# The place of two pairs' x loads on one core's DMA queue: four layers on a graph of 2048 nodes

## The chip, the core and the metric

The kernel runs on one core of a Trainium2 chip. Five engines work side by side, each through its own instructions in their written order, and wait for each other by semaphores: PE (TensorE, matrix products), DVE (VectorE), ACT (ScalarE), POOL (GpSimd) and SP (SyncE, which only issues transfers here). Transfers (DMAs) between the chip's memory (HBM) and the core's own memory (SBUF) are issued by SP, ACT or POOL and share 16 DMA engines. The metric is the device time of one execution in microseconds (us).

## The reference

Four layers work on `x`, of 8 batches x 2048 nodes x 64 channels, with one adjacency matrix `adj` of 2048 x 2048 (each row sums to 1). After each layer comes `x = layernorm(x + layer(x))`.

```python
# layer 0: node-wise weights made from an embedding of 16 numbers
w = einsum('nd,dkio->nkio', embedding, weight); b = einsum('nd,do->no', embedding, bias)
x_g = [x, adj @ x, 2 * adj @ (adj @ x) - x]          # k = 0, 1, 2
out = einsum('bnki,nkio->bno', x_g, w) + b
# layer 1: attention over the graph
e = leaky(s1[:, :, None] + s2[:, None, :]); att = softmax(where(adj > 0.5, e, -9e15))
out = elu(att @ x)
# layer 2: (adj + I) @ (x W^T + b) / degree
# layer 3: three steps of  v = relu([v, adj @ v] W1^T + b1) W2^T + b2
```

Everything is fp32. The host hands `adj` over twice, as it is (`adj`) and transposed (`adj_t`), and `x` with the nodes as rows.

## The kernel before

The 8 batches are four pairs; a pair's x is one SBUF buffer `SX[p]` of 128 partitions x 16 node tiles x 128 (two batches x 64 channels). It is loaded by `load_x(p, c, eng)` in four pieces of 256 KB, one for each quarter c of the nodes, and later overwritten by the results of each layer.

A product with adj is a sweep (`sweep`): for each of four column quarters, PE multiplies 16 tiles of a source by eight `a` tiles of adj (512 KB each), gathering in `acc`. The tiles come through a ring of six buffers; `fetch` issues the next load on SP when PE has let go of a buffer. Sweep 0 makes y1 = adj x for pairs 0 and 1. Sweep 1 makes adj y1 for pair 0 (`acc<-a,SA`). Sweep 2 does it for pair 1 (`acc<-a,SB`) and, with the same `a` tiles, makes y1 of pair 2 (`acc<-a,SX`): its first product, `first_product(2)`. Sweep 3 does the same for pairs 2 and 3. Later sweeps belong to layers 2 and 3.

Between the products stands the rest of layer 0: `second_pass` multiplies the stacked terms by the weights (`yp`; a group is six matmuls, for one node tile and one half of the 16 embedding numbers), and `add_terms` scales and adds the halves on ACT and DVE (`terms`). For pair 0 ACT takes the first half and DVE the second. PE can't begin a group before ACT or DVE has emptied the bank (PSUM) that it writes.

Beside all this the rows of adj go through the core once, for layer 1's mask and layer 2's degree: `rows_of_adj` loads 16 row tiles `an` of 1 MB on SP into a ring of four buffers; ACT sums each (L483), DVE makes the mask `mr` (L489) and POOL stores it (`by_row`).

`constants()` loads what is small, on SP: the first weights, then x of pairs 2 and 3 (`load_x` at L330, written by the helper's line L277 in the profile), then 17 small loads for layers 2 and 3 (L340 to L346: `w2bd`, `w31v`, `w31e`, `w32bd`, `w32c` twice each, `b2b`, `b32b`, `b31b` and `b32c` twice each, `ivc`). `weights_of_l23` makes the later weights from these on DVE, PE (`ps_w`) and ACT.

The order on every engine is fixed when the program is built. Each piece of work is a generator that yields the engine it needs next and what it waits for; a planner (`Plan`) holds an estimated time for each engine and for DMA and always goes on with the piece that can begin first by that estimate. `yield "PE", [180.0]` means: not before the planner's clock for this reaches 180. Planned times are close to the chip's, not equal: what is planned at 180 is issued on SP at 191.5 us. On the chip only semaphores hold; each engine goes through its list in order. SP's transfers use eight semaphores in turn, so that one issue waits for the landing of the eighth before it.

Of the kernel before, what the change touches and what calls it, by code (L numbers as in the profile page):

```python
# [20 lines left out]
NCH = 4  # L21
# [6 lines left out]
NPAIR = B // 2  # L28
# [125 lines left out]
def mm(cols, n=1):  # L154

    return n * max(4 * cols / 2390, 0.224)


def tr(n=1):
    return 0.11 * n  # L160
# [6 lines left out]
def act(n, k=1):  # L167
    return k * (n / 1220 + 0.14)
# [3 lines left out]
def resnorm_d4_kernel(  # L172
# [21 lines left out]
    nc = tc.nc  # L194
    plan = Plan()
    at = plan.at
# [27 lines left out]
    def tiny(shape, name, bufs=4):  # L224
        return wp.tile(shape, F32, tag=name, name=name, bufs=bufs)

    def tiles(c):
        return slice(c * TPC, (c + 1) * TPC)

    def cols(c):  # L230
        return slice(c * CW, (c + 1) * CW)
# [12 lines left out]
    SX = [slots.tile([P, NT, P], F32, name=f"SX{p}") for p in range(NPAIR)]  # L244
# [31 lines left out]
    def load_x(p, c, eng):  # L276
        eng.dma_start(  # L277
            SX[p][:, tiles(c), :],
            x[cols(c), p * P : (p + 1) * P].rearrange("(t p) n -> p t n", p=P),
        )  # L280
# [28 lines left out]
    def constants():  # L309

        yield "PE", [40.0]
        nc.sync.dma_start(emb_sb, emb.rearrange("(t p) d -> p t d", p=P))
        nc.sync.dma_start(bias_sb, bias0)
        nc.sync.dma_start(embT, emb_t)
        halves = [slice(0, C), slice(C, P)]
        for k, w in enumerate((wk0, wk1, wk2)):
            for h in halves:
                nc.sync.dma_start(w[h, :], w0[k * C : (k + 1) * C, :])
        for k in range(2):
            for e in range(2):  # L320
                nc.sync.dma_start(a4[halves[e], 2 * k + e : 2 * k + e + 1], a1[halves[k], :])
        yield "PE", [70.0]
        nc.vector.tensor_tensor(wk0, wk0, wk2, ALU.subtract)
        nc.vector.tensor_scalar_mul(wk2, wk2, 2.0)
        plan.run("DVE", 2.0)
        plan.start(0, embedding_bias())
        yield "PE", [180.0]
        for p in range(2, NPAIR):
            for c in range(NCH):
                load_x(p, c, nc.sync)  # L330
        yield "PE", [220.0]
        for t, src in (
            (w2bd, w2t),
            (w31v, w31t[0:C, :]),
            (w31e, w31t[C:P, :]),
            (w32bd, w32t),
            (w32c, w32t),
        ):
            for h in halves:
                nc.sync.dma_start(t[h, h], src)  # L340
        nc.sync.dma_start(b2b, b2.to_broadcast([P, C]))
        nc.sync.dma_start(b32b, b32.to_broadcast([P, C]))
        for h in halves:
            nc.sync.dma_start(b31b[h, :], b31)
            nc.sync.dma_start(b32c[h, :], b32.rearrange("o c -> c o"))
        nc.sync.dma_start(ivc, iv)  # L346
        yield "PE", [260.0]
        plan.start(0, weights_of_l23())

# [36 lines left out]
    def copy(eng, dst, src):  # L388
        (nc.scalar.copy if eng == "ACT" else nc.vector.tensor_copy)(dst, src)

    def cost(eng, n, k=1):
        return (act if eng == "ACT" else dve)(n, k)
# [11 lines left out]
    def embedding_bias():  # L404
        yield "PE", [pp_ring]
        pe, k = pp_ring.take([P, NT, C], "ps_eb")
        for t in range(NT):
            nc.tensor.matmul(
                pe[:, t, :], lhsT=embT[:, t * P : (t + 1) * P], rhs=bias_sb, start=True, stop=True
            )  # L410
        done = plan.run("PE", mm(C, NT))
        eng = yield EITHER, [done, e_ring]
        sb, ke = e_ring.take([P, NT, C], "eb_sb")
        copy(eng, sb, pe)
        done = plan.run(eng, cost(eng, 1024), done)
        pp_ring.give(k, done)
        e_ring.give(embT_k, plan.free["PE"])
        for e in range(2):
            nc.gpsimd.dma_start(eb[:, :, e, :], sb)
            done = plan.dma("DMA", 512, done)  # L420
        e_ring.give(ke, done)
        at["eb"] = done

    def weights_of_l23():


        yield "DVE", []
        for w, blocks in ((w2bd, 2), (w32c, 2), (b2b, 1), (b32b, 1)):
            mean = tiny([P, 1], "w_mean", 2)
            nc.vector.tensor_reduce(mean, w, AX.X, ALU.add)  # L430
            nc.vector.tensor_scalar_mul(mean, mean, 1.0 / C)
            for e in range(blocks):
                rows = slice(e * C, (e + 1) * C) if blocks == 2 else slice(0, P)
                block = w[rows, e * C : (e + 1) * C]
                nc.vector.tensor_scalar(block, block, mean[rows], None, ALU.subtract)
        plan.run("DVE", 3.0)

        nc.vector.tensor_tensor(w31v, w31v, w31e, ALU.subtract)

        yield "PE", [pp_ring, yt_ring]  # L440
        w32d, k2 = yt_ring.take([P, CW], "w32d")
        pw, k = pp_ring.take([P, CW], "ps_w")
        nc.tensor.transpose(pw[:, 0:P], w32bd, ident)
        nc.scalar.copy(w32d[:, 0:P], pw[:, 0:P])
        nc.vector.tensor_copy(w32d[:, P : 2 * P], b32c.to_broadcast([P, P]))
        done = plan.run("ACT", act(P), plan.run("PE", tr()))
        pp_ring.give(k, done)
        st_ring.give(w32bd_k, done)
        yield "PE", [pp_ring, done]
        pw, k = pp_ring.take([P, CW], "ps_w")  # L450
        for i, (lhs, rhs) in enumerate(
            [(w32d[:, 0:P], w31v), (w32d[:, 0:P], w31e), (w32d[:, P : 2 * P], w31e)]
        ):
            nc.tensor.matmul(
                pw[:, i * P : (i + 1) * P], lhsT=lhs, rhs=rhs, start=True, stop=True
            )
        nc.tensor.matmul(
            pw[:, 3 * P : 3 * P + 1], lhsT=w31v, rhs=b32c, start=True, stop=True
        )
        done = plan.run("PE", mm(P, 4))  # L460
        yield "ACT", [done]
        for i, dst in enumerate((gv, ge, ceb)):
            nc.scalar.copy(dst, pw[:, i * P : (i + 1) * P])
        nc.scalar.activation(b31n, pw[:, 3 * P : 3 * P + 1], AF.Identity, bias=b31b)
        done = plan.run("ACT", act(P, 4), done)
        pp_ring.give(k, done)
        yt_ring.give(k2, done)
# [93 lines left out]
    def y1_of(p):  # L561
        return (SA, SB)[p % 2]

    def y1_chunk(p, c, pa, ka, done):
        eng = yield EITHER, [done, yt_ring]
        yT, ky = yt_ring.take([P, CW], "y1T")
        copy(eng, yT, pa)
        done = plan.run(eng, cost(eng, CW), done)
        acc_ring.give(ka, done)
        nc.gpsimd.dma_start(y1_cols[p][:, cols(c)], yT)  # L570
        stored = plan.dma("DMA", 256, done)
        at["y1T", p, c] = stored
        yield "PE", [done, pp_ring]
        pt, k = pp_ring.take([P, TPC, P], "ps_y1")
        for j in range(TPC):
            nc.tensor.transpose(pt[:, j, :], yT[:, j * P : (j + 1) * P], ident)
        done = plan.run("PE", tr(TPC), done)
        yt_ring.give(ky, max(done, stored))
        eng = yield EITHER, [done]
        copy(eng, y1_of(p)[:, tiles(c), :], pt)  # L580
        done = plan.run(eng, cost(eng, CW), done)
        pp_ring.give(k, done)
        at["y1", p, c] = done
# [541 lines left out]
    def product(source, evict, need=None, before=None, seed=None):  # L1125
        return source, evict, need or (lambda q: []), before or (lambda c: []), seed
# [302 lines left out]
        at["joined", p] = 0.0  # L1429

    def first_product(p):
        return product(SX[p], lambda c, *a: y1_chunk(p, c, *a))

    def second_product(p):
        return product(
# [19 lines left out]
    def sweeps():  # L1455
# [13 lines left out]
        for s in range(3):  # L1469
            order_of_joint()  # L1470
        refill()
        yield from sweep(first_product(0), first_product(1), masks=True)
        for p in range(NPAIR):
            products = [second_product(p)]
            if 0 < p < NPAIR - 1:
                products.append(first_product(p + 1))
            if p == NPAIR - 1:
                yield from sweep(layer2_product(0))
                at["x1 used"] = 0.0
            yield from sweep(*products)  # L1480
# [16 lines left out]

    ctx.enter_context(tc.manual_schedule())
    plan.start(0, constants())
    plan.start(1, rows_of_adj())  # L1500
    plan.start(1, sums_of_a())
# [45 lines left out]
```

## Time and profile before

| what | value |
|---|---|
| median of three runs | 2073.46 us (2072.73 to 2073.87) |
| the profiled execution | 2070.24 us |
| its span, first to last instruction | 2068.5 us |
| mean granted clock of TensorE | 0.994 |
| DMA, whole span | 522.80 MB, mean 253 GB/s |

The profile is of one execution. Its span is cut into 40 slices; the clock granted to PE is 9 tenths or more in all of them, but within a slice it can fall to half for some microseconds. A queue's issue is where the instruction stands on SP; the landing is when its semaphore is full. Busy shares of DMA by 10 us stretches around the moved loads (start to end, share of the 16 engines, GB/s):

| stretch, us | DMA share | GB/s |
|---|---|---|
| 170 to 180 | 0.31 | 90 |
| 180 to 190 | 0.86 | 259 |
| 190 to 200 | 1.06 | 390 |
| 200 to 210 | 1.11 | 349 |
| 210 to 220 | 1.03 | 414 |
| 220 to 230 | 1.02 | 351 |
| 230 to 240 | 1.05 | 416 |
| 240 to 250 | 0.44 | 159 |
| 250 to 260 | 0.74 | 267 |
| 260 to 270 | 1.00 | 346 |
| 270 to 280 | 0.85 | 301 |
| 280 to 290 | 0.18 | 55 |
| 290 to 300 | 0.13 | 52 |

[...]

### The profile page before, as it was taken

Reading aid. Unit: us, or ns where it says so; the run is one execution under the profiler, and the core shown is the slowest. Engines: PE = TensorE matmul, PEld = TensorE weight load, DVE = VectorE, ACT = ScalarE, POOL = GpSimd, SP = SyncE. Lnnn points to the kernel's source line nnn. Section 1 sums busy time; section 2 is a strip of 40 time slices with the busy share of each in tenths; the row PEclk is TensorE's granted clock in tenths of the full one; section 3 lists DMA queues with packets and bytes.
Section 4 is the critical chain, followed back from the end, with each engine's and each line's share of the span. In section 5 each row is a group of like instructions: output and inputs, shape, how many; then the busy total and the mean of one; then the engine's idle time right before and its main releaser. Section 6 shows DMA issues by size and latency. Waiting matters only on the chain.

```text
span 2068.5 us, 22208 instructions
## 1 busy us (share of the span) xinstructions
PE 2020.9 (98%) x7841; PEld 876.3 (42%) x7841; DVE 1469.3 (71%) x1893; ACT 978.0 (47%) x1786; POOL 301.7 (15%) x488
## 2 busy tenths in 40 slices
PE   8999999999999999999999999999999999999997
PEld 3434444444343343344433343443333454444444
DVE  2225665998799999988999989999989832121224
ACT  0014544268777657758765737623767521000002
POOL 2220101112223232232001101001101000000000
PEclk9999999999999999999999999999999999999999
DMA  9798855766668779898548779679878678888885
GB/s 305 259 341 299 325 182 195 252 220 183 147 218 199 215 233 307 307 258 270 187 154 305 259 269 320 231 266 363 277 241 276 206 243 258 273 267 265 266 287 183
DMA packets 207041, 522.80 MB, mean 253 GB/s; under 512 B 22274, under 2 KB 30594, under 8 KB 202818
## 3 DMA queue, kind: packets, MB, share of 16 engines
q1 hardware_dynamic: 151026, 352.34, 50.6%
q0 software_dynamic: 51680, 166.95, 26.7%
q10 hardware_dynamic: 4224, 2.10, 0.4%
q8 instruction: 62, 1.02, 0.2%
q14 instruction: 49, 0.40, 0.1%
HBM read 488.61 MB, written 64.16 MB: 267 GB/s over the span
## 4 chain that ended last, share of the span: by engine, by line
PE 84%; issue 5%; DMA 5%; DVE 4%; ACT 1%; POOL 0%; SPq 0%; POOLq 0%; ACTq 0%; DVEq 0%
PE acc L401 53%; PE yp L653 15%; PE po L882 10%; DMA a<-in_adj_t 3%; DMA an<-in_adj 2%; PE ps_u L401 2%; DVE e L855 1%; PE ps_emb L401 1%; PE pf L401 1%; DVE e L868 1%; PE ps_sv L401 1%; PE ps_v L401 0%; PE ps_xg L607 0%; PE ps_vT L1064 0%; PE ps_xT L717 0%
## 5 line engine op out<-in xcount | busy, mean ns | idle before, releaser
L401 PE MATMUL acc<-a,SX 128*128 128x512 f32 (+1 forms) x1376 | 493.7, 597 | 10.0 <-DMA SX<-in_x 6.7
L401 PE MATMUL acc<-a,SB 128*128 128x512 f32 (+1 forms) x1096 | 378.2, 595 | 3.6 <-DMA a<-a_plus_i 2.3
L863 ACT ACTIVATE e<-e,sv 128x1024 f32<-128x1024 f32 x256 | 280.2, 1152 | 90.8 <-DVE e L855 88.0
L677 ACT ACTIVATE terms<-yp,emb_sb 128x128 f32<-128x128 f32 x896 | 243.3, 396 | 149.9 <-PE yp L653 149.6
L401 PEld LDWEIGHTS acc<-a,SX 128*128 128x128 f32 (+1 forms) x1376 | 189.6, 169 | 270.6 <-issue 252.9
L868 DVE TENSOR_TENSOR e<-e,mb 128x2048 f32<-128x2048 f32 x128 | 291.0, 2285 | 9.0 <-ACT e L863 8.7
L855 DVE TENSOR_TENSOR e<-s1b,mk 128x2048 f32<-128x2048 f32 x128 | 290.2, 2285 | 5.9 <-PE po L882 2.9
L777 DVE CUSTOM_DVE_ANT_0 junk<-s2b,mr 128x2048 bf16<-128x2048 f32 x128 | 292.8, 2287 | 1.8
L871 ACT ACTIVATE e<-e 128x2048 f32<-128x2048 f32 x128 | 245.9, 1931 | 77.9 <-DVE e L868 77.8
L882 PE MATMUL po<-e,SX 128*64 128x512 f32 x1024 | 231.9, 595 | 0.0
L401 PEld LDWEIGHTS acc<-a,SB 128*128 128x128 f32 (+1 forms) x1096 | 141.1, 164 | 200.5 <-issue 191.6
L401 PE MATMUL acc<-a,SA 128*128 128x512 f32 (+1 forms) x396 | 181.7, 611 | 4.8 <-DMA a<-in_adj_t 4.8
L689 DVE TENSOR_TENSOR terms<-terms 128x512 f32<-128x512 f32 (+1 forms) x176 | 130.0, 738 | 42.4 <-ACT terms L677 38.3
L653 PE MATMUL yp<-SH,xgT 64*128 64x512 f32 x512 | 138.2, 616 | 3.2 <-ACT terms L677 3.1
L850 POOL DMA_DIRECT2D mk<-by_col x128 | 70.8, 560 | 463.1 <-DVE e L855 413.8
L882 PEld LDWEIGHTS po<-e,SX 128*64 128x64 f32 x1024 | 70.7, 137 | 145.8 <-issue 138.6
L653 PE MATMUL yp<-wk,xgT 64*128 64x512 f32 x512 | 131.2, 589 | 0.0
L653 PE MATMUL yp<-SH,y2T 64*128 64x512 f32 x512 | 131.2, 589 | 0.0
L401 PEld LDWEIGHTS acc<-a,SA 128*128 128x128 f32 (+1 forms) x396 | 71.7, 192 | 97.2 <-issue 87.5
L401 PE MATMUL acc<-a,ut 128*64 128x512 f32 (+1 forms) x276 | 87.0, 594 | 2.0 <-DVE wk L1295 2.0
L401 PE MATMUL acc<-a,t 128*128 128x512 f32 x192 | 85.4, 592 | 0.0
L1120 POOL DMA_DIRECT2D out<-SX x12 | 9.1, 755 | 467.2 <-DVE SX L555 428.3
(248 smaller groups left out, 1726.3 us busy)
## 6 DMA issues: line engine op xcount, KB each, us to landing
a<-in_adj_t SPq DMA_DIRECT2D x384, 512.0 KB, 5.8
a<-a_plus_i SPq DMA_DIRECT2D x88, 512.0 KB, 5.2
mr<-by_row POOLq DMA_DIRECT2D x64, 512.0 KB, 6.0
mk<-by_col POOLq DMA_DIRECT2D x128, 256.0 KB, 5.6
a<-sb SPq DMA_DIRECT2D x40, 512.0 KB, 4.4
a<-sc SPq DMA_DIRECT2D x40, 512.0 KB, 4.4
a<-sd SPq DMA_DIRECT2D x40, 512.0 KB, 4.7
a<-sa SPq DMA_DIRECT2D x40, 512.0 KB, 4.3
```

Of the source, the lines that this page charges most:

```text
L401: nc.tensor.matmul(out[h], lhsT=lhsT[:, h], rhs=rhs, skip_group_check=True, **kw)
L653: nc.tensor.matmul(yp[:, e, :], lhsT=v[rows, cs], rhs=w[rows, hs], start=(k3 == 0), stop=(k3 == 2),)
L677: nc.scalar.activation(batches(terms[0][:, dd, :]), term, AF.Copy, scale=weight)
L689: nc.vector.tensor_tensor(a, a, b, ALU.add)
L777: nc.vector.tensor_tensor_reduce(out=junk, in0=s2b[e][0], in1=masks[t][0], scale=1.0, scalar=LOWEST, op0=ALU.add, op1=ALU.max, accum_out=m ...
L850: nc.gpsimd.dma_start(mk, by_col[jt // 2][:, jt % 2, h * HALF : (h + 1) * HALF])
L855: nc.vector.tensor_tensor(e, s1b[0], mk.unsqueeze(1).to_broadcast([P, 2, HALF]), ALU.add)
L863: nc.scalar.activation(e[:, i, :], e[:, i, :], AF.Prelu, bias=sv[:, 2 + i, jt : jt + 1], alpha=ALPHA)
L868: nc.vector.tensor_tensor(e, e, mb[0], ALU.add)
L871: nc.scalar.activation(e, e, AF.Exp)
L882: nc.tensor.matmul(po[i * C : (i + 1) * C, f, :], lhsT=SX[p][:, t, i * C : (i + 1) * C], rhs=e[:, i, f * CW : (f + 1) * CW], start=(t == 0 ...
L1120: nc.gpsimd.dma_start(out[cols(c), p * P : (p + 1) * P].rearrange("(t p) n -> p t n", p=P), v)
```

## The change

The eight loads of x for pairs 2 and 3 leave their place in `constants()` and go to its end, each pair with a due time of its own on SP's planned clock, 270 and 430. The planner is told of them (256 KB each on SP), and `first_product` of pairs 2 and 3 now waits in the plan for the landing; before, the plan knew of neither. On the chip a semaphore holds PE in both kernels. The due time 220 of the small weight loads goes as well, so they follow at 180.

```diff
         yield "PE", [180.0]
-        for p in range(2, NPAIR):
-            for c in range(NCH):
-                load_x(p, c, nc.sync)
-        yield "PE", [220.0]
         for t, src in (
             (w2bd, w2t),
...
         yield "PE", [260.0]
         plan.start(0, weights_of_l23())
+        for p in range(2, NPAIR):
+            yield "SP", [(270.0, 430.0)[p - 2]]
+            for c in range(NCH):
+                load_x(p, c, nc.sync)
+                at["x", p] = plan.dma("SP", 256)
...
     def first_product(p):
-        return product(SX[p], lambda c, *a: y1_chunk(p, c, *a))
+        return product(
+            SX[p],
+            lambda c, *a: y1_chunk(p, c, *a),
+            need=lambda q: [("x", p)] if p > 1 else [],
+        )
```

The programs hold the same instructions. Their order on SP differs as said, and by what the planner makes of it there: after the sixth `an` and nine `a` follow the 17 small loads, then `an` 7 to 9, `a`, `an` 10, `a`, `an` 11, six `a`, `an` 12 to 15, seven `a`, `an` 16, x of pair 2, 28 `a`, x of pair 3. Before, it was the eight x, `an` 7 to 9, `a`, `an` 10, `a`, `an` 11, six `a`, `an` 12 and 13, the small loads, `an` 14 and 15, seven `a`, `an` 16, 58 `a`. At the start of sweep 2 PE does six groups of `yp` (both halves of three node tiles) before the first `acc<-a,SX`, which stood ahead of them, and `ps_w` comes after the first two groups. On ACT the sixteenth row tile and one group of `terms` change places with the copies of `ps_w`; on DVE one group of `terms` comes ahead of that tile's mask.

## The prediction

> **What bounds the kernel now.** I read the page's busy times and chain first, then who PE (TensorE) waits for, then the chain and the queue of SP (SyncE) around the moved loads, then PE's clock in short stretches.
>
> ```profile
> PE 2020.9 (98%) x7841; PEld 876.3 (42%) x7841; DVE 1469.3 (71%) x1893; ACT 978.0 (47%) x1786; POOL 301.7 (15%) x488
> ...
> PE 84%; issue 5%; DMA 5%; DVE 4%; ACT 1%; POOL 0%; SPq 0%; POOLq 0%; ACTq 0%; DVEq 0%
> ```
>
> PE is busy 98% of the span and is 84% of the chain. What PE loses by waiting is the end's loss, and little is lost. The change touches loads issued after 191 us, so I asked what PE waits for from 190 to 300 us (total, times, longest):
>
> ```profile
> PE ps_xg L607 <- ACT terms L677: 3.6, 1, 3.6
> PE yp L653 <- ACT terms L677: 1.4, 1, 1.4
> PE ps_w L454 <- issue: 1.3, 1, 1.3
> ```
>
> Three waits, at 212.04, 257.94 and 282.22 us. The chain in the same stretch (start, length, what) says what stands behind the first two:
>
> ```profile
> 202.44 6.89 DMA an<-in_adj
> ...
> 209.35 2.00 ACT an L483 x2
> ...
> 230.90 14.04 DMA an<-in_adj
> 244.96 0.47 SPq L340
> ...
> 250.89 6.48 DMA an<-in_adj
> ...
> 259.45 2.07 ACT terms L677 x8
> ...
> 261.56 1.12 PE ps_xg L607 x4
> ```
>
> ScalarE works in order: a row tile `an` (1 MB of adj) that lands late holds up the `terms` behind it, and PE waits for the bank that those free. From 230.90 to 250.89 the delay is SP's: the small weight loads (L340 to L346) go out one by one, each after the landing of the DMA eight before it on that queue, and two row tiles queue behind them. SP's own timeline at the moved loads:
>
> ```profile
> 189.35 2.08 SPq L271 DMA_DIRECT2D a<-in_adj_t  x2
> 191.48 10.85 SPq L277 DMA_DIRECT2D SX<-in_x  x8
> 202.44 1.67 SPq L476 DMA_DIRECT2D an<-in_adj  x3
> ```
>
> And the clock (stretch, its length, PE busy, weight loads, DVE, ACT, POOL, then PEclk, DMA share, GB/s):
>
> ```profile
> 137.38:140.80 3.42, 0.91 (x3) 0.08 (x1) 1.78 (x5) 0.00 (x0) 1.71 (x4) 1.00 1.04 385
> 140.80:147.62 6.82, 6.19 (x7) 2.35 (x8) 0.00 (x0) 0.00 (x0) 1.00 (x2) 0.50 1.00 295
> 256.85:260.26 3.41, 1.09 (x3) 0.19 (x1) 0.74 (x3) 2.81 (x6) 0.00 (x0) 1.00 0.99 406
> 260.26:267.09 6.83, 5.53 (x10) 2.93 (x11) 6.56 (x19) 4.27 (x9) 1.95 (x3) 0.50 1.05 381
> 212.47:215.89 3.42, 2.43 (x12) 1.25 (x14) 2.98 (x12) 3.42 (x7) 0.53 (x1) 1.00 1.05 417
> ...
> 1246.70:1250.12 3.42, 1.68 (x4) 0.38 (x2) 3.42 (x4) 2.95 (x3) 0.54 (x1) 1.00 0.85 296
> ```
>
> Where PE idled 73% or 68% of such a stretch, 6.83 us at half clock followed. Idle 29% or 51%, none did. So the wait at 257.94 cost 3.62 us and then half of 5.53 us of work: 2.76 us.
>
> **The change, part by part.** The built program's order on each engine shows what moves. No instruction comes or goes. On SP, the eight x loads leave their place after the `a` of 191.06 us. But the wait "220" goes with them, so the 17 small weight loads now stand there, ahead of the seventh `an`, where the x loads were. The last four `an` before the final one go out in one run. x of pair 2 stands after the sixteenth `an`, x of pair 3 after 28 more `a`. On PE, in sweep 2, the first product with pair 2 moves behind six groups of `yp`, and `ps_w` behind two. DVE and ACT move one group each, POOL none.
>
> *The seventh row tile.* The eighth small load waits for the `a` of 191.06. Its landing lies one x tile (0.90 us, the spacing of the x landings) before the first x landing at 200.60: 199.7. From the eighth small load to the next `an` SP took 250.89 - 244.96 = 5.93 us. So `an` goes out at 205.6, not 202.44. Its way was 6.89 us behind 2 MB of x; now that queue is empty. Upper end: those 6.89, landing at 212.5. Lower end: an `a` of half the size alone took 3.6 us, plus 1.2 for the second half (two row tiles behind the x landed 2.5 us apart): 4.8, landing at 210.4. The row at 250.89, behind the same small loads, took 6.48 beside a 512 KB store; I take 6.0, so 211.6 against 209.32: **+2.3 us** (1.1 to 3.2). ACT and PE follow it one for one, as ACT starts that tile 0.03 us after landing.
>
> *The clock behind it.* PE idles from 212.04 to 213.46 + 2.3 = 215.8, 3.7 us, as long as the two waits that were followed by half clock. In the stretch 212.47 to 215.89 it idles 97%. Half of 6.83 us is 3.4, half of the two busy times seen 3.1 and 2.8: **+3.0 us** (0 to 3.4). From here PE is 5.3 us late.
>
> By the rows 2.3 us of idling within one stretch is already enough (68%). The Trainium skill ("TensorE: Matmul & The Clock Gate", "Why this matters for your kernels") sets the limit higher: it warns of PE gaps above about 3 us. At the tile's lower end the gap is 1.42 + 1.1 = 2.5 us: by the skill that is free and the sum -6.6, by the rows it may pay and the sum is -3.6. The trace's three long gaps, 1.42, 3.14 and 3.62 us, fit both.
>
> *The wait at 257.94.* The fourteenth `an` no longer stands behind small loads. With PE 5.3 late the last `a` before the run goes out at 229.85 + 5.3 = 235.2, then four row tiles at 0.5 us each; their buffers were freed by 230.5. The twelfth took 11.8 us in a full queue, the rest follow at 2.5 to 2.9 us: landings at 247, 250, 252.7, 255.5 at the latest. ACT takes the fourteenth by 255 and `terms` by 259; PE needs them at 257.94 + 5.3 = 263.2. Wait and clock go: **-3.62 - 2.76 = -6.4 us** (0 if the row tiles were 4 us later still).
>
> *The wait at 282.22* (`ps_w` on DVE's weight work, 279.79 to 283.5): two `yp` groups, 5.15 us, now lie in between. **-1.27** (0 to -1.27).
>
> *The new wait on x.* Pair 2 goes out near 272.5 behind the last `an` (landed 280.69) and four x tiles of 0.9 us: all by 284.5. PE starts sweep 2 near 277.4 and then does 1.8 of `acc`, six groups of 2.58 and the `ps_w`: first use at 295.7. 11 us of cover, the six `yp` groups; without them it would be about 3 us. The `a` tile held meanwhile delays the next `a` from 282.3 to about 297, which is needed five tiles of 3.44 us later: free. Pair 3 goes out near 448 and is used from 491.3: free. Behind each burst only `a` wait on SP, for PE anyway.
>
> **Sum:** 2.3 + 3.0 - 6.4 - 1.3 = -2.4 us. Nothing after 330 us has a time of its own: orders are the same and DVE's long stage starts from `ps_rows`, which moves along. Against the profiled execution (2070.24 us, 1.7 around the span of 2068.5) that makes 2067.8. The runs' median lies 3.2 higher, 2073.46; against it 2071.1.
>
> **Rivals.**
>
> 1. *The gap at 212 stays short of the clock's limit*, because `an` lands by 210.4 or the stretches lie so that none is 68% idle. For: the lower end above gives a gap of 2.5 us, and stretches beginning elsewhere can split 3.7 us in two parts under 2.3 (about a quarter of positions). Against: with the stretches of this trace 97% idle. Time: without the 3.0, -5.4, 2068.1; with +1.1, -6.6, 2066.9.
>
> The skill's same page ("What's actually happening") calls those stretches free-running, so their place may differ from run to run; no run here shows that yet.
>
> 2. *The small loads are slow in their new place* (the other side). For: the x loads issued there took 10.85 us for 8, 1.36 each, against 0.59 for the ten small ones ahead of 250.89. At 1.36, 17 small ones end at 214.6; `an` lands at 220.6, 11.3 late, PE idles 12.7 us and pays the clock: 11.3 + 3.4 - 7.7 = +7.0, 2080.5. Against: the x rows wait on landings that end at 199.7. It decides from `an` 4.7 us late (issued after 208): from there the kernel is not faster.
>
> 3. *PE waits for x in sweep 2.* For: x comes on the same queue as `a`. Against: 11 us of cover. If SP held the x loads until the buffer freed at 297, they'd land at 303, a wait of 7 us and the clock, 3.4: -2.4 + 10.4 = +8.0, 2081.5.
>
> The Trainium skill ("DMA: Bandwidth & Descriptors", "Rules for kernel authors") has it that a DMA is issued early and waited for late, which speaks against this change; by it alone this rival is the result.
>
> 4. *The change does nothing at the end*: PE's gain at 258 is lost to a wait later, as the row tiles pace ACT whatever the order: 0, 2073.5.
>
> **How the numbers follow.** Forecast 0.42, rival 1 0.34, rival 2 0.16, rival 3 0.03, rival 4 0.05. What a measurement here can tell from no change is about 0.2%, 4.1 us. Faster by more: rival 1 and 0.04 of the forecast's low end, 0.38. Slower by more: rivals 2 and 3, less 0.01 near zero, 0.18. Within: 0.44. The forecast's own range is 2068 to 2074 (1.1 to 3.2 for the tile, 2.8 to 3.4 for the clock, 0 to 1.3 for `ps_w`). The whole range reaches to rival 1's low end, 2066.5, and over half of rival 2, 2077.5.
>
> **What would show it.** SP: 17 small loads from 191.5, seventh `an` out near 205.6, landed near 211.6. PE: a wait for ACT's `terms` of some 3.7 us ending near 215.8, 6.83 us of half clock behind it; no wait at `ps_xg` near 263 and full clock there; no wait at `ps_w`; none on `SX<-in_x` after the start. I am wrong if the half clock stays away, if the seventh tile goes out after 208, or if `ps_xg` still waits.

## The result, and the profile after

| what | before | after |
|---|---|---|
| median beside each other, 14 runs each | 2073.00 us (2070.15 to 2077.51) | 2068.71 us (2063.54 to 2072.39) |
| the profiled execution | 2070.24 us | 2070.71 us |
| its span | 2068.5 us | 2068.9 us |
| mean granted clock in it | 0.994 | 0.992 |
| 64th `acc<-a,SA` to 64th `acc<-a,SB` on PE | 186.19 us | 181.92 us |
| from there to the end | 1693.56 us | 1698.75 us |

The changed kernel takes 0.9979 of the time before (95% interval 0.9970 to 0.9987): 4.3 us less, where 2.4 less was forecast. The two profiled executions don't show that: they end within half a microsecond of each other. So I cut each at two matmuls that all orders share, the 64th of `acc<-a,SA` (188.72 us before) and the 64th of `acc<-a,SB` (374.91). The stretch between them holds everything that the change moves on PE up to there, and is called "the stretch" from here on. It is 4.27 us shorter. The rest is 5.19 us longer, though its instructions are the same in the same order. The first number is the change. The second has to be explained too.

Who PE waits for from 190 to 300 us in the changed kernel (total, times, longest) is one line, where it was three:

```profile
PE yp L654 <- ACT terms L678: 3.4, 1, 3.4
```

The waits at `ps_xg` and at `ps_w` are gone, no wait on x has come, and the one for `terms` has grown from 1.4 to 3.4 us. The chain of the same stretch (start, length, what):

```profile
190.61 8.83 DMA a<-in_adj_t
199.44 0.01 issue
199.45 0.47 SPq L336
...
204.78 0.49 SPq L342
...
205.37 5.48 DMA an<-in_adj
210.85 0.02 issue
210.87 2.00 ACT an L484 x2
212.88 2.07 ACT terms L678 x8
214.94 0.04 issue
214.99 7.12 PE yp L654 x24
```

The eighth small load stands until the `a` before it has landed at 199.44, nine more follow at some 0.6 us each, and only then does the seventh row tile go out. ScalarE takes it 0.02 us after landing; its `terms` end at 214.94, and PE, idle since 211.59, goes on at 214.99. The 24 matmuls behind take 7.12 us, where the same 24 take 5.35 elsewhere in this chain. SP's timeline shows the two other places (start, length, line, what, how many):

```profile
233.53 3.03 SPq L477 DMA_DIRECT2D an<-in_adj  x4
257.76 11.11 SPq L271 DMA_DIRECT2D a<-in_adj_t  x7
268.97 0.49 SPq L477 DMA_DIRECT2D an<-in_adj  x1
269.51 6.83 SPq L277 DMA_DIRECT2D SX<-in_x  x4
```

The twelfth to the fifteenth row tile go out together, and ScalarE is ahead of PE at `ps_xg` (261.16). The four x tiles land at 280.3 to 282.9; PE first multiplies by them at 294.1.

The clock of the changed kernel (stretch, length, PE busy, weight loads, DVE, ACT, POOL, then PEclk, DMA share, GB/s) explains both numbers:

```profile
212.06:215.47 3.41, 0.48 (x2) 0.30 (x4) 2.53 (x8) 3.41 (x11) 0.53 (x1) 1.00 1.00 416
215.47:218.89 3.42, 3.42 (x10) 1.37 (x8) 2.98 (x8) 3.24 (x4) 0.26 (x1) 0.50 1.03 368
683.10:686.51 3.41, 1.34 (x7) 0.26 (x4) 3.41 (x4) 3.41 (x5) 0.00 (x0) 1.00 0.96 267
686.51:689.93 3.42, 3.42 (x8) 1.86 (x9) 3.42 (x2) 3.42 (x4) 2.69 (x5) 0.50 0.79 251
1355.53:1358.94 3.41, 1.11 (x9) 0.89 (x9) 3.34 (x5) 1.22 (x2) 0.00 (x0) 1.00 0.80 261
1358.94:1365.77 6.83, 6.16 (x18) 3.78 (x17) 6.41 (x11) 1.11 (x4) 0.53 (x1) 0.50 0.28 89
```

and the kernel before at the same matmuls as the third and fourth line:

```profile
686.93:690.34 3.41, 2.12 (x10) 0.43 (x6) 3.41 (x2) 3.41 (x5) 0.00 (x0) 1.00 0.94 241
690.34:693.75 3.41, 2.62 (x9) 1.45 (x10) 3.41 (x4) 3.41 (x5) 2.38 (x5) 1.00 0.85 270
```

PE waits 2.07 us there in both kernels (689.05 before, 684.33 after). Before, a border of the 3.41 us stretches cuts that wait in two, 1.29 and 0.79 us, and the clock stays. After, it lies in one, and half clock follows. The same happens at 1356, and at 1656 behind a stretch that is 48% idle. Four stretches at half clock, with 13 us of work in them, are what the first profile had not. At full clock that work takes 6.5 us less. Waits for `a` tiles differ as well: from 1416 to 1434 they are 1.3 us shorter in sum (the longest, at 1418, is 1.04 us instead of 1.80), from 813 to 822 they are 0.5 us longer. That comes to 5.7; the other 0.5 us down to 5.19 is not assigned. Whether the four stretches belong to the change or to the run was tried below.

### The profile page after: what moved, and what is told of

It is laid out like the page before. It is cut to its first block, busy times and chain, and to the rows that moved or that the text cites. A ratio compares the mean times of both kernels' runs of the same rounds, so it can differ in the third digit from the quotient of the medians.

```text
span 2068.9 us, 22205 instructions
## 1 busy us (share of the span) xinstructions
PE 2024.9 (98%) x7841; PEld 879.4 (43%) x7841; DVE 1469.5 (71%) x1893; ACT 977.4 (47%) x1786; POOL 302.7 (15%) x488
## 4 chain that ended last, share of the span: by engine, by line
PE 85%; issue 5%; DMA 4%; DVE 4%; ACT 1%; SPq 1%; POOL 0%; POOLq 0%; DVEq 0%; ACTq 0%
PE acc L402 54%; PE yp L654 16%; PE po L883 10%; DMA a<-in_adj_t 2%; PE ps_u L402 2%; DVE e L856 1%; PE ps_emb L402 1%; DMA a<-a_plus_i 1%; PE pf L402 1%; DVE e L869 1%; PE ps_sv L402 1%; PE ps_v L402 0%; DMA wk<-in_w 0%; PE ps_vT L1065 0%; PE ps_xT L718 0%
```

## The experiments

Theory: the gain comes from the *order on SP*. The 17 small loads no longer stand ahead of the fourteenth and fifteenth row tile; part of it is given back because they now stand ahead of the seventh. Rival: the gain comes from the *transfers*, the 2 MB of x that no longer fill the queues from 200 to 210 us. The diff moves both at once, so the first four kernels, timed beside the same runs of the kernel before, set each by itself. All four have PE, DVE and ACT orders equal to those of before (x early) or after (x late), and differ on SP alone. What the expectations call the stretch "from the last to the last" is the stretch defined above, from the 64th to the 64th. It differs by 0.9 us between two profiles of the kernel before and by 0.6 us between two of the changed one; of every other kernel there is one profile.

**x late alone.** Against the changed kernel:

```diff
-        yield "PE", [180.0]
+        yield "PE", [220.0]
         for t, src in (
```

> x of pairs 2 and 3 late as in the changed kernel, the due time 220 of the small loads put back, so that they stand ahead of `an` 14 and 15 again. Theory (the order on SP: the gain comes from the small loads leaving their place ahead of `an` 14 and 15): `an` 7 goes out at 191.5 and its wait (1.42 us) goes, the `ps_w` wait (1.27) goes, the wait at `ps_xg` near 258 and its half clock (3.62 + 2.76) stay: -2.7 us against before. Rival (the full queue: what gains is the 2 MB of x that no longer lie in front of the row tiles, some 7.2 us of transfers): the small loads, which wait for landings, are through some 7 us sooner, more than the 3.6 us that the wait lasted, so that wait and its half clock go too: -9.1 us.

Measured: 2070.91 us against 2073.88, ratio 0.9981 (0.9969 to 0.9993); the stretch 181.39, -4.80. Who PE waits for, 190 to 330 us:

```profile
PE ps_xg L608 <- ACT terms L678: 2.8, 1, 2.8
```

and SP's timeline:

```profile
229.40 1.12 SPq L336 DMA_DIRECT2D w2bd<-in_w2t  x2
...
246.93 0.50 SPq L342 DMA_DIRECT2D ivc<-in_iv  x1
247.54 0.83 SPq L477 DMA_DIRECT2D an<-in_adj  x2
```

The wait that the theory put on the order is still there. The transfers count, but little there: with x gone the fourteenth row tile goes out at 247.54 instead of 250.89, 3.35 us sooner, but it took 0.57 longer on its way, and PE arrives 1.92 sooner too. So the wait shrinks by 0.85 us (3.62 to 2.77), and only one stretch at half clock follows: -1.42 - 1.27 - 0.85 - 1.06 = -4.6. The rival's -9.1 is excluded. The theory's -2.7 was too small a gain, by those 0.85 and 1.06 us, which it had put at nothing.

**The small loads early alone.** Against the kernel before:

```diff
                 load_x(p, c, nc.sync)
-        yield "PE", [220.0]
         for t, src in (
```

> x where it was, the due time 220 dropped: the 17 small loads follow right behind the eight x, ahead of `an` 7 to 9. Both theories of the place agree on the first part: eight of the small loads wait for the x landings (the last near 207), nine more at 0.6 us each, so `an` 7 goes out near 212.4 and lands near 218.3 instead of 209.3; PE waits some 10.3 us near 212 instead of 1.4 and pays half a clock window (3.0) behind it. Then the theory of the order has the wait at 258 gone (-6.4): +5.5 us against before. The theory of the full queue leaves it there unless PE is simply too late to meet it.

Measured: 2076.65 us against 2073.88, ratio 1.0012 (1.0002 to 1.0022); the stretch 191.00, +4.81. The seventh row tile went out at 213.41. PE's waits:

```profile
PE yp L652 <- ACT terms L676: 10.3, 1, 10.3
PE ps_w L453 <- DVE w32d L444: 1.3, 1, 1.3
```

As expected, the wait near 212 is 10.26 us and the sum is on the wrong side (the medians show 2.8 us of it). The wait at 258 is gone, but that decides nothing: PE comes to its `ps_xg` at 268.8 there, where before it wanted to begin it at 257.9, and that alone may cover the row tile, as the expectation allowed. Half of the diff by itself makes the kernel slower; it is x's leaving that makes room for the small loads.

So the theory is not borne out as it was put. x late alone gives as much as the whole diff (-4.80 and -4.27 in the stretch, 3.0 and 4.3 us in the medians, with intervals that overlap). With x late, what the small loads' earlier place saves at 258 is given back at 212; with x early, that place costs 4.8 us. Whether x's leaving counts by its eight places in SP's list or by its 2 MB was not separated.

**The small loads away, x late and x early.** Against the changed kernel, and (x put back at 180) against the kernel before, the small loads go to the planned time 70, ahead of every row tile; they are issued from 68.8 to 79.3 us:

```diff
         plan.start(0, embedding_bias())
-        yield "PE", [180.0]
         for t, src in (
```

> x late as in the changed kernel, the small loads at 70 on the planner's clock, ahead of every row tile. By the theory of the order no row tile is held by a small load: the waits near 212 (1.42), 258 (3.62 and 2.76 of half clock) and at `ps_w` (1.27) all go, -9.1 us against before and -4.8 against the changed kernel, about 2064. The rival that the half clock falls anywhere in a run, whatever the waits near 200 to 300, has it at the changed kernel's time, about 2069.

> x where it was, the small loads at 70 on the planner's clock, ahead of every row tile. By the theory of the order the wait at 258 goes with its half clock though x keeps its place (-6.4 us); the waits near 212 (1.42) and at `ps_w` (1.27) stay: about 2066.6. By the theory of the full queue `an` 14 lands as late as before behind the 2 MB of x and the wait at 258 stays: 0, about 2073.

Measured with x late: 2062.69 us, ratio 0.9941 (0.9927 to 0.9956), the stretch 176.75, -9.44. With x early: 2067.44 us, ratio 0.9969 (0.9956 to 0.9981), the stretch 179.78, -6.41. With x late PE has no wait at all from 190 to 330; the busy time of 188 to 330 us (length, then PE busy first):

```profile
188.00:330.00 142.00, 142.00 (x539) 64.57 (x539) 79.08 (x228) 62.98 (x170) 14.85 (x24) 1.00 0.79 277
```

With x early two waits stay, as expected:

```profile
PE ps_w L453 <- DVE w32d L444: 1.3, 1, 1.3
PE yp L652 <- ACT terms L676: 1.2, 1, 1.2
```

The wait at 258 is gone though all of x still stands ahead of the seventh row tile and those behind it: it needs the small loads. This run bears the theory out on that wait. What x's place is worth when they are out of the way is 3.0 us in the stretch, most of it these two waits. With x late and the small loads away the kernel beats both. Whether the small loads cost anything near 70 is not settled: the 64th `acc<-a,SA` starts at 190.0 there, in ten profiles of all kernels between 187.9 and 190.0.

**The small loads from POOL.** Is it their place in SP's list or their transfer that holds up the seventh row tile? Against the changed kernel:

```diff
-                nc.sync.dma_start(t[h, h], src)
+                nc.gpsimd.dma_start(t[h, h], src)
```

and so for all 17.

> The changed kernel with the 17 small loads issued by POOL instead of SP, at the same planned time: their bytes cross at the same moment as the seventh row tile, but SP has nothing to issue ahead of it. Stretch from the last `acc<-a,SA` to the last `acc<-a,SB` of that sweep: 186.2 us before, 181.9 in the changed kernel, 176.8 with the loads at 70. Theory (what costs is the queue position: SP issues them one by one, each after the landing of the eighth before): `an` 7 goes out near 191.5, no wait near 212 nor 258, the stretch is 177 us, -9 against before. Rival (what costs is their transfers, many small packets that slow the row tile): `an` 7 still lands after 210 and PE waits near 212 with half clock behind it, stretch 180 to 182, -4 to -6.

Measured: 2065.90 us against 2072.95, ratio 0.9961 (0.9948 to 0.9974); the stretch 176.75, no wait on PE from 190 to 330. POOL's timeline, then SP's:

```profile
188.17 1.08 POOL L336 DMA_DIRECT2D w2bd<-in_w2t  x2
...
201.14 0.52 POOL L342 DMA_DIRECT2D ivc<-in_iv  x1 [0.23 <-DMA w32c<-in_w32t]
```

```profile
191.74 1.48 SPq L477 DMA_DIRECT2D an<-in_adj  x3
```

The same loads at nearly the same time, taking 13.5 us on POOL, cost PE nothing: the seventh row tile goes out at 191.74. What costs is what stands behind them in their engine's list. That their transfers are free is not shown: the row tile took 12.31 us on its way, against 10.49 with x late alone, but landed at 204.04, before ScalarE came to it (204.67). The Trainium skill ("DMA: Bandwidth & Descriptors", "Rules for kernel authors") says of spreading transfers over engines that it brings no bandwidth and "only saves sequencer issue time"; the trace agrees that SP's time is what is saved, and here that time, with SP's waiting for landings in it, was the whole price. What spreading does to bandwidth no run here shows.

**The planner not told of x.** Against the kernel with both away (x of pair 2 due at 262 instead of 270, which keeps its place on SP):

```diff
     def first_product(p):
         return product(
             SX[p],
             lambda c, *a: y1_chunk(p, c, *a),
-            need=lambda q: [("x", p)] if p > 1 else [],
         )
```

> x late and the small loads at 70 (due time 262 for x of pair 2, which gives the same SP order as before it), but the planner is not told that the first products wait for x, so that PE begins sweep 2 with pair 2 ahead of the `yp` groups, as in the kernel before. Theory (the planned wait is what gives the cover): PE reaches the first `acc<-a,SX` near 273.9, x lands near 276.6: a wait of 2.8 us on x and one window of half clock behind it (1.7, bounds 0 and 3.4): +4.5 us against the run with both away, stretch 181. Rival (x is in time without it): no wait, stretch 177.

Measured: 2068.61 us against 2072.95, ratio 0.9975 (0.9966 to 0.9984); the stretch 181.73, 4.98 more than with both away. PE's waits, then its clock:

```profile
PE acc L401 <- DMA SX<-in_x: 3.1, 1, 3.1
```

```profile
272.50:275.91 3.41, 1.05 (x3) 0.57 (x4) 3.14 (x14) 0.00 (x0) 0.00 (x0) 1.00 1.09 289
275.91:279.33 3.42, 3.42 (x13) 2.38 (x13) 0.53 (x2) 0.15 (x1) 0.00 (x0) 0.50 0.23 71
```

3.10 of wait and half of 3.42 make 4.8 of the 4.98. The diff's last part, which adds no instruction, is worth as much here as the whole diff gains: without the six `yp` groups ahead, x is late.

**Both kernels once more, for a second profile.**

> The changed kernel once more, for a second profile. Theory (the half-clock windows lie on a grid of 3.41 us that runs free of the kernel, and a wait pays if it empties some 0.55 to 0.6 of one window): the waits near 212, 684, 1246, 1356 and 1656 are as long as in its first profile, and the windows behind them differ wherever the grid cuts the wait otherwise; the length from the last `acc<-a,SB` of sweep 2 to the end lies between 1693 and 1699 us (1693.6 in the profile before, 1698.8 in that after). Rival (the change itself brings the half clock of the later stages): the four later windows come again at the same waits and that length is 1698.8.

> The kernel before once more, for a second profile. Theory (free grid): the waits at 212, 258 and 282 are 1.4, 3.6 and 1.3 us again, and some of the waits near 689, 1246, 1356 and 1657, free in its first profile, may be followed by half clock now: from the last `acc<-a,SB` of sweep 2 to the end 1693 to 1699 us. Rival: no half clock after 267 and 1693.6 again.

Measured: from the 64th `acc<-a,SB` to the end 1694.34 us (after, 1698.75 the first time) and 1698.63 (before, 1693.56 the first time). The two have changed places. In the second profile of the changed kernel the wait at 684 was followed by half clock again, those at 1355 and 1654 were not:

```profile
1353.20:1356.61 3.41, 1.87 (x5) 0.57 (x3) 3.24 (x10) 1.26 (x4) 0.00 (x0) 1.00 0.53 175
1356.61:1360.03 3.42, 1.99 (x13) 1.59 (x14) 3.38 (x5) 1.40 (x4) 0.00 (x0) 1.00 0.41 132
1653.57:1656.98 3.41, 1.76 (x9) 0.78 (x8) 2.76 (x9) 1.69 (x5) 0.00 (x0) 1.00 0.76 252
1656.98:1660.39 3.41, 3.41 (x21) 2.45 (x20) 2.75 (x8) 1.08 (x3) 0.00 (x0) 1.00 0.17 58
```

In the second one of the kernel before, half clock stood behind the waits at 691, 1252 and 1363, four stretches that its first profile had not. So the give-back belongs to the run, not to the change. The expectations missed in one thing: the waits themselves are not fixed. The one at 212 was 2.78 us, not 3.40, and the one at 258 before was 5.40, not 3.62. PE's waits before, second profile, and its clock:

```profile
PE ps_xg L607 <- ACT terms L677: 5.4, 1, 5.4
```

```profile
257.18:260.60 3.42, 1.65 (x4) 0.38 (x2) 0.00 (x0) 0.50 (x1) 0.00 (x0) 1.00 0.99 412
260.60:264.01 3.41, 0.00 (x0) 0.00 (x0) 1.83 (x5) 3.41 (x10) 0.10 (x1) 1.00 1.01 406
264.01:267.42 3.41, 3.20 (x7) 1.92 (x8) 3.27 (x11) 2.21 (x3) 1.85 (x3) 0.50 1.04 388
```

A longer wait, but one stretch at half clock instead of two: 5.40 + 1.60 = 7.0 against 3.62 + 2.76 = 6.4. Why the row tile took 7.46 us on its way this time, not 6.48, and went out 1.67 later, was not pursued.

The stretch in all ten profiles, in us, by where the small loads and x stand:

| small loads | x early | x late |
|---|---|---|
| behind `an` 13 | 186.19 and 187.11 (before) | 181.39 |
| ahead of `an` 7 | 191.00 | 181.92 and 181.31 (after) |
| ahead of all `an` | 179.78 | 176.75; planner not told 181.73 |
| on POOL | not tried | 176.75 |

## Why the prediction was nearly right

- **The seventh row tile** (+2.3 us): out at 205.37 (205.6 predicted), landed 210.85 (211.6), PE's wait 3.40 instead of 1.42: +1.98. Its bounds came from the two neighbouring ways; the 5.48 us that it took lay between them.
- **The clock behind it** (+3.0): the term that was mis-sized. It measured 7.12 - 5.35 = +1.77, and one stretch again in the second profile. The prediction took 6.83 us of half clock for granted because the two cases that it read had it. In both of these PE still waited in the first stretch at half clock (19% and 38% idle), and that bought the second one. Here the wait ended 0.48 us before the border, PE was busy through the next stretch, and full clock came back after 3.41.
- **The wait at 258** (-6.4): as predicted, -3.62 - 2.76 in these two profiles. The runs with x late alone and with the small loads away put it on the small loads, as the prediction had it; that x late alone would shorten it too (by 0.85 us, and 1.06 of clock) it did not have.
- **The wait at `ps_w`** (-1.27): as predicted.
- **No wait on x**: x in place by 282.9 (284.5 predicted), used from 294.1 (295.7). The price without the cover, "about 3 us", was 3.10 and its clock, measured in the kernel with the small loads away. x of pair 3 landed by 460.1 and was first used at 484.3; the 491.3 of the prediction is a row of `acc<-a,SA`, which changes nothing.
- **The sum**: the measured steps give 1.98 + 1.77 - 6.38 - 1.27 = -3.9; the stretch shows -4.27, of which 0.4 is not assigned; the medians -4.3. The 2.4 us by which the predicted 2071.1 was too high are 1.2 of clock, 0.3 of row tile, 0.4 not assigned, and 0.5 that the median of before was lower this time (2073.0 for 2073.5).
- **The range**: the low end of the forecast's own range, 2068, is not what its terms give: 1.1 + 2.8 - 6.4 - 1.3 = -3.8, which is 2069.7. The measured 2068.71 lies below that, since the clock's 1.77 lies below 2.8, and nearer to the first rival's 2068.1 than to 2071.1. That it falls inside the forecast's range as written is luck; the steps, but for the size of that one, are not.
- **"Nothing after 330 us has a time of its own"** fits the medians (4.3 us less, 4.27 in the stretch) and fails for a single profile: from the 64th `acc<-a,SB` to the end it is 1693.4 to 1698.8 us in ten profiles, whatever the kernel.

Of the rivals, the first (no half clock at 212) did not come, though the cost of it came out between that and the forecast. The second did not come: the 17 loads took 14.2 us, 0.84 each instead of 1.36, and the seventh row tile went out 2.9 us later than before, not 4.7. It did go out at 213.41, with 8.8 us of wait more, where x still stood ahead, but not because the small loads were slow: they took 10.7 us there (202.65 to 213.30). The third, PE waiting for x, did not come with the change; it came where the planner was not told, with the small loads away. The fourth did not come: no wait followed in the stretch, and the ratio's interval, 0.9970 to 0.9987, does not reach 1. The rule of the Trainium skill that the prediction weighed with the third ("DMA: Bandwidth & Descriptors", "Rules for kernel authors"), to issue a DMA early, did not decide: x of pair 2, issued 74 to 78 us later, is the faster version in all three pairs of the table, with other work planned ahead of its use.

## What to carry to other kernels

A load that nobody waits for can still cost, by what stands behind it in its engine's list: put many small loads where that list holds nothing urgent, or on an idle engine. Before moving a transfer, take the diff apart: here one half alone was slower, the other alone gave as much as both, which is half the gain of the best version, and the best was a place that the change did not try. Where PE's waits are near 2 us, compare medians or stretches between shared instructions, since two single profiles differ by more than such a change brings.

## What the runs showed of the hardware

- Half clock comes in whole stretches of 3.413 us. The first full-clock stretch starts 9.6 to 12.8 us into the span, differently in each of the ten profiles, and all others follow on that grid. Behind every stretch at full clock in which PE was idle 61% or more stood one at half clock; behind none of 46% or less, from 100 us on. Between 48% and 58% both occurred. A stretch at half clock was followed by full clock where PE was idle 15% of it or less, and by another at half where it was idle 19% or more.
- So one and the same wait of 2.07 us (680 to 694 us) was followed by half clock in five profiles of ten. The Trainium skill ("TensorE: Matmul & The Clock Gate", "Why this matters for your kernels") warns of gaps above about 3 us; these rows put the limit lower, at some 2 us within one stretch. The same page of the Trainium skill ("What's actually happening") calls the stretches free-running; the ten different starts agree.
- Before 100 us the idle share is not the whole rule. Near 75 us PE runs 32 small matmuls (`ps_eb`, 16 x 64) for 3.8 us. The profile shows PE busy throughout, yet half clock followed in the eight profiles in which they filled 71% or more of one stretch, and not in the two in which they filled 62% or less.
- Seventeen loads of 32 KB and less, in the same order, occupied SP for 10.5 us where almost no landing had to be waited for (68.8 to 79.3), for 14.2 in the changed kernel (191.03 to 205.27) and for 19.0 before (231.82 to 250.78). Some 0.6 us each is the issue; the rest is waiting for the landing of the transfer eight before. The DMA engines were about as busy each time (share 0.66, 0.58 and 0.70).
